# Two passes over the last four tiles of a projection stage

## The chip, the cores and the metric

The kernel runs on one core of a Trainium2 chip, as one program in one launch. The time is device time in microseconds (us), from three runs: a median of 3396.61 us, between 3395.56 and 3397.88. The engines are TensorE (PE: matmul; PEld: weight load), VectorE (DVE), ScalarE (ACT), GpSimd (POOL) and SyncE (SP, which here only starts transfers). Sixteen DMA engines move data between memory and the core's buffers; they are fed from a queue of SP (q1) and one of GpSimd (q0).

## The reference, cut to what matters

`z` is the input, of shape (1, 384, 384, 128). Two layers follow each other; all is float32.

```python
# layer 0
z_n = layernorm(z, norm_g, norm_b)
a = linear(z_n, Wa, ba) * sigmoid(linear(z_n, Wga, bga))
b = linear(z_n, Wb, bb) * sigmoid(linear(z_n, Wgb, bgb))
x = einsum('bijd,bjkd->bikd', a, b)
x = layernorm(x, normo_g, normo_b)
z1 = z + linear(x, Wo, bo) * sigmoid(linear(z_n, Wgo, bgo))
# layer 1 (pair = z1)
left = pair @ W_left + b_left + pair @ W_eq + b_eq
right_sum = sum(pair @ W_right + b_right, axis=2)
gate = sigmoid(pair @ W_gate + b_gate)
out = (left * right_sum * gate) @ W_out + b_out
return layernorm(out + pair, ln_scale, ln_bias)
```

## The kernel before

The kernel has three stages. The order of the instructions on each engine is the order in which the program writes them (`manual_schedule`, L37).

**Projection** (L93 to L321). x is cut into NT = 72 tiles of 128 rows by 16 columns (CX), each tile into four chunks of 4 columns (CT), so a step `s` (L183) handles one chunk and there are 288 steps. A step works on chunk `s` in its matmuls and on later chunks in the rest:

- `fetch` (L104) loads x three tiles ahead into a pool of four buffers (tag xt), on SP's queue; `statistics` (L121) takes mean and variance two tiles ahead on VectorE; `norm_factors` (L128) makes scale and offset one tile ahead on GpSimd; `normalise` (L139) writes zn on ScalarE, three chunks ahead.
- `turn` (L157) transposes the next chunk on TensorE into PSUM (ptr); `turned_out` (L166) copies it on ScalarE to zT.
- Four projections, `proj` (L199), of 128 x 512 each: ga, a, gb, b; `sigmoid` (L204) on ScalarE makes sga and sgb. VectorE forms at = (pa + bias) * sga (L218) and bt = (pb + bias) * sgb (L229). Four small matmuls pgo (L234) and gs (L236) make the output gate's argument; its sigmoid is taken one step later in `gate` (L173).
- All projections share a ring of six PSUM buffers (tag pk). The results at, gt, zb and bt have two buffers each.

Stores: at the end of a tile A is written from at (L222), and G from gt (L180), both from GpSimd's queue; Z, the input plus a bias, is made and written by GpSimd in `residual` (L149). B is written differently: bt gathers 64 columns, that is four tiles, and is written in four pieces of 32 rows (L243 to L249) on SP's queue. A piece goes out at the end of each tile; at the end of the last tile all pieces that are left go out at once (L245), these are the four of the last group.

**Product** (L387 to L452). For each of the 128 channels d, ad and bd are read back from A and B (`fetch`, L394; both on SP's queue, six channels ahead), multiplied (L412), and X, with running sums s1 and s2, is kept. s1 and s2 are cleared by GpSimd ahead of the stage (L332, L333).

**Output** (L457 to L593). The layer norm, the gate and layer 1, in a pipeline over rows.

The first product can start only when A and B are complete, since ad and bd of any channel hold values of every tile.

Of the kernel before, what the change touches and what calls it, by code (L numbers as in the profile page):

```python
# [8 lines left out]
FP = mybir.dt.float32  # L9
AF = mybir.ActivationFunctionType  # L10
# [9 lines left out]
def kernel(ctx: ExitStack, tc: tile.TileContext, ins, out: bass.AP):  # L20
# [66 lines left out]

    CG, CX, CT, BR = 64, 16, 4, 32  # L90
    TS = CX // CT
    NT = NB * (N // CX)
    with tc.tile_pool(name="wprep", bufs=6) as wp, tc.tile_pool(name="p1x", bufs=4) as px, tc.tile_pool(name="p1s", bufs=3) as ps, tc.tile_pool(  # L93
        name="p1o", bufs=2
    ) as po, tc.tile_pool(name="p1t", bufs=2, space=PSUM) as ppt, tc.tile_pool(
# [4 lines left out]
        def place(n):  # L100
            rb, c = divmod(n, N // CX)
            return rb * P, c * CX

        def fetch(n, parts=1):  # L104
            if n >= NT:
                return
            r0, c0 = place(n)
            xt = px.tile([P, CX, C], FP, tag="xt", name=f"xt_{n}")
            for k in range(0, CX, CX // parts):
                nc.sync.dma_start(  # L110
                    out=xt[:, k : k + CX // parts, :], in_=x[r0 : r0 + P, c0 + k : c0 + k + CX // parts, :]
                )
            tiles[n] = {
                "x": xt,
                "st": ps.tile([P, CX, 6], FP, tag="st", name=f"st_{n}"),
                "mv": ps.tile([P, CX, 2], FP, tag="mv", name=f"mv_{n}"),
                "rstd": ps.tile([P, CX], FP, tag="rstd", name=f"rstd_{n}"),
                "off": ps.tile([P, CX], FP, tag="off", name=f"off_{n}"),
            }
# [19 lines left out]
        def normalise(n, t, cs=range(CT)):  # L139
            if n >= NT:  # L140
                return
            g = tiles[n]
            for c in (t * CT + k for k in cs):
                nc.scalar.activation(  # L144
                    g["zn"][:, c, :], g["x"][:, c, :], AF.Identity,
                    bias=g["off"][:, c : c + 1], scale=g["rstd"][:, c : c + 1],
                )
# [9 lines left out]
        def turn(s):  # L157
            n, t = divmod(s, TS)
            if n >= NT:
                return  # L160
            ptr = ppt.tile([P, CT, P], FP, tag="ptr", name=f"ptr_{s}")
            for c in range(CT):
                nc.tensor.transpose(ptr[:, c, :], tiles[n]["zn"][:, t * CT + c, :], ident)  # L163
            turned[s] = ptr

        def turned_out(s):  # L166
            if s // TS >= NT:
                return
            zT = ps.tile([P, CT, P], FP, tag="zT", name=f"zT_{s}")
            nc.scalar.copy(zT, turned[s])  # L170
            turned[s] = zT

        def gate(s):  # L173
            n, t = divmod(s, TS)
            gs = gated.pop(s)
            gt = tiles[n]["gt"]
            nc.scalar.activation(gt[:, t * CT : (t + 1) * CT, :], gs, AF.Sigmoid)
            if t == TS - 1:
                r0, c0 = place(n)
                nc.gpsimd.dma_start(out=G[r0 : r0 + P, c0 : c0 + CX, :], in_=gt)  # L180
                tiles.pop(n - 1, None)

        def step(s):  # L183
            n, t = divmod(s, TS)
            r0, c0 = place(n)
            if t == 0:
                fetch(n + 3)
                if n:
                    norm_factors(n + 1)
                tiles[n]["at"] = po.tile([P, CX, P], FP, tag="at", name=f"at_{n}")  # L190
                tiles[n]["gt"] = po.tile([P, CX, C], FP, tag="gt", name=f"gt_{n}")
                if c0 % CG == 0:
                    bts[n // (CG // CX)] = po.tile([P, P, CG], FP, tag="bt", name=f"bt_{n}")
            at, bt = tiles[n]["at"], bts[n // (CG // CX)]
            k0 = c0 % CG + t * CT
            zT = turned.pop(s)
            ahead = (n + 1, t - 1) if t else (n, TS - 1)

            def proj(k):  # L199
                pk = ppp.tile([P, CT, P], FP, tag="pk", name=f"p{k}_{s}")  # L200
                nc.tensor.matmul(pk, lhsT=wT[k], rhs=zT, start=True, stop=True)  # L201
                return pk

            def sigmoid(k, pg):  # L204
                sg = ps.tile([P, CT, P], FP, tag="sg", name=f"sg{k}_{s}")
                nc.scalar.activation(sg, pg, AF.Sigmoid, bias=bcol["g" + k])  # L206
                return sg

            if n == 0:
                statistics(1, t)  # L210
                norm_factors(1, t * CT, t * CT + CT)
            statistics(n + 2, t)
            pga, pa = proj("ga"), proj("a")
            sga = sigmoid("a", pga)
            if s:
                gate(s - 1)
            normalise(*ahead, range(CT // 2))
            nc.vector.scalar_tensor_tensor(  # L218
                at[:, t * CT : (t + 1) * CT, :], pa, bcol["a"], sga, ALU.add, ALU.mult
            )  # L220
            if t == TS - 1:
                nc.gpsimd.dma_start(out=A[:, c0 : c0 + CX, r0 : r0 + P], in_=at)  # L222
            pgb = proj("gb")
            sgb = sigmoid("b", pgb)
            turn(s + 1)
            turned_out(s + 1)
            normalise(*ahead, range(CT // 2, CT))
            pb = proj("b")
            nc.vector.scalar_tensor_tensor(  # L229
                bt[:, :, k0 : k0 + CT].rearrange("d r c -> d c r"), pb, bcol["b"], sgb, ALU.add, ALU.mult  # L230
            )
            pgo = ppp.tile([P, CT, C], FP, tag="pk", name=f"pgo_{s}")
            for c in range(CT):
                nc.tensor.matmul(pgo[:, c, :], lhsT=zT[:, c, :], rhs=wT["go"], start=True, stop=True)  # L234
            gs = ps.tile([P, CT, C], FP, tag="gs", name=f"gs_{s}")
            nc.vector.tensor_tensor(gs, pgo, over(gate_bias, CT), ALU.add)  # L236
            gated[s] = gs
            if n == 1 and t < 3:
                residual(t)
            if n > 1 and t == 1:  # L240
                residual(n + 1)
            if k0 + CT == CG:
                b_out_of.extend((bt, r0, c0 + CX - CG, k) for k in range(0, P, BR))  # L243
            if t == TS - 1:
                store_b(len(b_out_of) if n == NT - 1 else 1)  # L245

        def store_b(pieces):
            for bt, r0, k0, r in b_out_of[:pieces]:
                nc.sync.dma_start(out=B[:, r0 + r : r0 + r + BR, k0 : k0 + CG], in_=bt[:, r : r + BR, :])  # L249
            del b_out_of[:pieces]  # L250
# [54 lines left out]
            if t == 1:  # L305
                prepare("go")
        for s in range(NT * TS):
            step(s)
            if s == TS:
                nc.vector.tensor_copy(ob_w, ob.to_broadcast([P, P]))  # L310
                prepare("o")
                nc.vector.tensor_scalar(center, ident, -1.0 / C, None, ALU.add)
                pc = ppp.tile([P, CT, P], FP, tag="pk", name="pc")[:, 0, :]
                nc.tensor.matmul(pc, lhsT=center, rhs=wT["o"], start=True, stop=True)
                nc.vector.tensor_copy(w_o0, pc)
                nc.vector.tensor_copy(w_o0[0:1, :], o_bias[0:1, :])
                nc.vector.tensor_tensor(w_left, w_left, w_eq, ALU.add)
                nc.vector.tensor_tensor(b_left, b_left, b_eq, ALU.add)
                nc.vector.tensor_scalar(b_right, b_right, float(N), None, ALU.mult)
                nc.vector.tensor_scalar(b_off, b_off, -1.0, None, ALU.mult)  # L320
        gate(NT * TS - 1)  # L321

# [4 lines left out]

    sums = ctx.enter_context(tc.tile_pool(name="sums", bufs=1, reuse_waits="tile"))  # L330
    x0, s1, s2, rs0 = (sums.tile([P, NB, N], FP, tag=k, name=k) for k in ("x0", "s1", "s2", "rs0"))
    nc.gpsimd.memset(s1, 0.0)  # L332
    nc.gpsimd.memset(s2, 0.0)  # L333
    LAST, AHEAD, R = 8, 6, 4
    pl = ctx.enter_context(tc.tile_pool(name="p3l", bufs=3, reuse_waits="tile"))
    group = {}
# [50 lines left out]
    with tc.tile_pool(name="p2", bufs=LAST, reuse_waits="tile") as p2, tc.tile_pool(  # L387
# [6 lines left out]
        def fetch(d):  # L394
            if d >= C:
                return
            ad = p2.tile([P, NB, N], FP, tag="ad", name=f"ad_{d}")
            bd = p2.tile([P, NB, N], FP, tag="bd", name=f"bd_{d}")
            nc.sync.dma_start(out=ad, in_=A[d].rearrange("(q p) i -> p q i", p=P))
            nc.sync.dma_start(out=bd, in_=B[d].rearrange("(q p) k -> p q k", p=P))  # L400
            factors[d] = ad, bd

# [26 lines left out]

        for d in range(AHEAD):  # L430
            fetch(d)
        for d in range(C - LAST):
            fetch(d + AHEAD)
            for ib in range(NB):
                product(d, ib)
# [194 lines left out]
```

## Time and profile before

| what | value |
|---|---|
| median of three runs | 3396.61 us |
| the profiled execution | 3399.26 us, its span 3397.5 us |
| PE busy | 3296.4 us (97% of the span) |
| DVE, ACT, POOL busy | 2673.1, 2307.0, 2089.3 us |
| mean granted TensorE clock | 0.988 |
| moved by DMA | 910.52 MB, 268 GB/s |
| one step on PE in the projection stage | 4.765 us |
| A, G, Z stores of 1 MB, median from issue to landing | 7.6, 8.8, 8.2 us |
| B store of 1 MB, median from issue to landing | 16.9 us |
| ad, bd loads, median from issue to landing | 7.3, 8.2 us |

The profile is one execution. Busy time is the time in which an engine has an instruction at work; a row of instructions has the line of the kernel, the engine, the operation and its tiles. A clock of 1.00 is TensorE's full speed. "Landing" is the end of a transfer, as the one who waits for it sees it. A DMA share of 1 means that all sixteen engines are busy. Rows of the timeline have their start and duration ahead, and behind, in brackets, what the engine waited for before.

### The profile page before, as it was taken

How to read it: one execution, taken by the hardware profiler on the slowest of the kernel's cores; microseconds unless marked ns; L12 is line 12 of the kernel's file. 1: busy time of each engine (PE TensorE's matmuls, PEld its weight loads, DVE VectorE, ACT ScalarE, POOL GpSimd, SP SyncE). 2: the span in 40 equal slices, each digit the busy share in tenths (PEclk: the TensorE clock that was granted, in tenths of full speed). 3: DMA queues.
4: the chain of work that ended last, by engine and by line, in shares of the span. 5: the costliest groups of instructions: out<-in, count | busy, mean ns of one | idle time of the engine just before them, and what ended most of it. 6: DMA issues, size and time to landing. Idle time of an engine off the chain costs nothing.

```text
span 3397.5 us, 53333 instructions
## 1 busy us (share of the span) xinstructions
PE 3296.4 (97%) x15581; PEld 2194.5 (65%) x15581; DVE 2673.1 (79%) x8605; ACT 2307.0 (68%) x5482; POOL 2089.3 (61%) x1562
## 2 busy tenths in 40 slices
PE   7999999999999999699999999899999999999997
PEld 4555555555555555355555555478888888888885
DVE  7777777777777777345555555599999999999998
ACT  5777877777877777422222222268888888888887
POOL 5555555555555555245555555338888888888887
PEclk9999999999999999899999999899999999999998
DMA  5888899999988899799999999667777777777773
GB/s 173 263 277 266 261 275 282 279 280 282 285 273 260 266 278 281 217 343 306 302 308 306 304 309 304 215 220 264 264 262 264 264 265 264 265 264 264 265 261 140
DMA packets 675330, 910.52 MB, mean 268 GB/s; under 512 B 319328, under 2 KB 616288, under 8 KB 647520
## 3 DMA queue, kind: packets, MB, share of 16 engines
q1 hardware_dynamic: 634000, 680.28, 63.4%
q0 software_dynamic: 40320, 226.51, 19.1%
q8 instruction: 126, 2.06, 0.2%
q14 instruction: 164, 1.34, 0.1%
q10 hardware_dynamic: 720, 0.33, 0.0%
HBM read 454.04 MB, written 452.98 MB: 267 GB/s over the span
## 4 chain that ended last, share of the span: by engine, by line
PE 91%; DVE 5%; POOL 1%; DMA 1%; issue 1%; SPq 0%; ACT 0%; POOLq 0%; ACTq 0%; DVEq 0%
PE pm L412 20%; PE pgo L234 7%; PE pga L201 7%; PE pa L201 7%; PE pgb L201 7%; PE pb L201 7%; PE pf L497 7%; PE py L507 7%; PE pleft L548 7%; PE pg L550 6%; PE ptr L163 4%; PE ptr L471 3%; DVE py L513 1%; DMA X<-xd 1%; DVE st L518 1%; DVE h L485 1%
## 5 line engine op out<-in xcount | busy, mean ns | idle before, releaser
L412 PE MATMUL pm<-bd,ad 128*128 128x384 f32 x2304 | 748.8, 489 | 32.0 <-DMA bd<-B 32.0
L412 PEld LDWEIGHTS pm<-bd,ad 128*128 128x128 f32 x2304 | 440.2, 191 | 339.2 <-issue 36.9
L427 POOL TENSOR_TENSOR s<-s,xd 128x384 f32<-128x384 f32 x381 | 380.3, 998 | 414.6 <-DVE xd L420 414.3
L425 ACT ACTIVATE sq<-xd 128x384 f32<-128x384 f32 x381 | 188.6, 495 | 566.0 <-DVE xd L420 566.0
L420 DVE TENSOR_TENSOR xd<-pm,x 128x384 f32<-128x384 f32 x381 | 212.2, 557 | 391.0 <-POOL s L427 321.6
L229 DVE SCALAR_TENSOR_TENSOR bt<-pb,c_L_conv_bb,sgb 128x512 f32<-128x512 f32 x288 | 321.0, 1115 | 247.6 <-ACT zT L170 239.1
L144 ACT ACTIVATE zn<-xt,off,rstd 128x128 f32<-128x128 f32 x1152 | 504.4, 489 | 15.1 <-POOL off L135 15.1
L540 ACT ACTIVATE res<-res,off,rs 128x128 f32<-128x128 f32 x1152 | 482.5, 486 | 18.4 <-POOL off L534 15.7
L513 DVE SCALAR_TENSOR_TENSOR py<-py,rs,gr 128x128 f32<-128x128 f32 x1152 | 431.4, 374 | 1.8 <-PE py L507 1.2
L222 POOL DMA_DIRECT2D A<-at x72 | 85.3, 1184 | 552.0 <-DVE at L218 552.0
L206 ACT ACTIVATE sga<-pga,c_L_conv_bga 128x512 f32<-128x512 f32 x288 | 197.9, 687 | 288.2 <-PE pga L201 288.2
L234 PEld LDWEIGHTS pgo<-wT_go,zT 128*128 128x128 f32 x2304 | 302.5, 192 | 137.7 <-issue 72.9
L518 DVE BATCH_NORM_STATS2 st<-res 128x6 f32<-128x128 f32 x1152 | 359.2, 313 | 0.3
L154 POOL TENSOR_TENSOR zb<-xt,r_L_conv_b_out 128x2048 f32<-128x2048 f32 x72 | 327.9, 4554 | 4.4 <-DMA Z<-zb 2.5
L580 POOL TENSOR_TENSOR res<-res,r_L_conv_ln_bias 128x1536 f32<-128x1536 f32 x94 | 324.7, 3455 | 7.4
L497 PE MATMUL pf<-w_o,h 128*128 128x128 f32 x2304 | 321.2, 276 | 6.1 <-ACT w_o L479 5.3
L579 POOL TENSOR_TENSOR res<-res,r_L_conv_ln_scale 128x1536 f32<-128x1536 f32 x94 | 325.4, 3461 | 0.1
L555 ACT ACTIVATE sg<-pg,c_L_conv_b_gate 128x384 f32<-128x384 f32 x384 | 223.0, 581 | 143.8 <-PE pg L550 90.9
L507 PE MATMUL py<-w_o,xr 128*128 128x128 f32 x2304 | 320.4, 275 | 0.0
L548 PE MATMUL pleft<-pairT,m_L_conv_W_left 128*128 128x384 f32 x768 | 313.0, 489 | 1.5 <-ACT pairT L473 1.3
L550 PE MATMUL pg<-pairT,m_L_conv_W_gate 128*128 128x384 f32 x768 | 311.1, 487 | 0.0
L125 DVE BATCH_NORM_STATS2 st<-xt 128x6 f32<-128x128 f32 x1152 | 305.6, 265 | 0.2 <-issue 0.2
(131 smaller groups left out, 6818.9 us busy)
## 6 DMA issues: line engine op xcount, KB each, us to landing
A<-at POOLq DMA_DIRECT2D x72, 1024.0 KB, 7.6
G<-gt POOLq DMA_DIRECT2D x72, 1024.0 KB, 8.8
Z<-zb POOLq DMA_DIRECT2D x72, 1024.0 KB, 8.2
B<-bt SPq DMA_DIRECT2D x72, 1024.0 KB, 16.9
ad<-A SPq DMA_DIRECT2D x128, 576.0 KB, 7.3
bd<-B SPq DMA_DIRECT2D x128, 576.0 KB, 8.2
xr<-X SPq DMA_DIRECT2D x96, 768.0 KB, 6.0
gr<-G SPq DMA_DIRECT2D x96, 768.0 KB, 7.6
```

The source lines that it names most:

```text
L144: nc.scalar.activation(g["zn"][:, c, :], g["x"][:, c, :], AF.Identity, bias=g["off"][:, c : c + 1], scale=g["rstd"][:, c : c + 1],)
L201: nc.tensor.matmul(pk, lhsT=wT[k], rhs=zT, start=True, stop=True)
L234: nc.tensor.matmul(pgo[:, c, :], lhsT=zT[:, c, :], rhs=wT["go"], start=True, stop=True)
L412: nc.tensor.matmul(pm, lhsT=ad[:, q, ib * P : (ib + 1) * P], rhs=bd[:, q, :], start=(q == 0), stop=(q == NB - 1),)
L427: nc.gpsimd.tensor_tensor(s1[:, ib, :], s1[:, ib, :], xd, ALU.add)
L497: nc.tensor.matmul(pf[:, q, :], lhsT=h[:, q * P : (q + 1) * P], rhs=w_o, start=True, stop=True)
L507: nc.tensor.matmul(py[:, q, :], lhsT=g["x"][:, i, q * P : (q + 1) * P], rhs=w_o0, start=True, stop=True)
L513: nc.vector.scalar_tensor_tensor(py[:, q, :], py[:, q, :], rs0[:, q, u : u + 1], g["g"][:, i, q, :], ALU.mult, ALU.mult)
L518: nc.vector.bn_stats(b["st"][:, k, q, :], b["res"][:, k, q, :])
L540: nc.scalar.activation(g["res"][:, i, q, :], g["res"][:, i, q, :], AF.Identity, bias=g["off"][:, i, q : q + 1], scale=g["rs"][:, i, q : q ...
L548: nc.tensor.matmul(pleft, lhsT=w_left, rhs=pairT, start=True, stop=True)
L550: nc.tensor.matmul(pg[:, 0:N], lhsT=w_gate, rhs=pairT, start=True, stop=True)
```

## The change

The last four tiles (68 to 71, the last group of B; steps S2 = 272 to 287) are handled in two passes. In the first pass each step does gb, b and the output gate, and the work ahead as before (statistics, factors, normalising, transposes), but neither ga nor a. The transposed chunk of these tiles is copied not into zT but into the tile's own x buffer, and stays there. After the first pass, whose end also sends off the B stores, the second pass runs ga and a for the 16 chunks from these buffers and stores A of the four tiles. The other 272 steps are written with new helper functions but keep their order.

Two more edits: ad of the first three channels (d below NB = 3) is read on GpSimd's queue in place of SP's, and the two clearings of s1 and s2 come after the first six fetches in the program.

```diff
+    S2 = (NT - CG // CX) * TS
...
         def turned_out(s):
             if s // TS >= NT:
                 return
-            zT = ps.tile([P, CT, P], FP, tag="zT", name=f"zT_{s}")
+            if s < S2:
+                zT = ps.tile([P, CT, P], FP, tag="zT", name=f"zT_{s}")
+            else:
+                n, t = divmod(s, TS)
+                zT = tiles[n]["x"][:, t * CT : (t + 1) * CT, :]
             nc.scalar.copy(zT, turned[s])
             turned[s] = zT
...
-                tiles.pop(n - 1, None)
...
+        def finish_a(s, pa, sga):
+            n, t = divmod(s, TS)
+            r0, c0 = place(n)
+            if t == 0:
+                tiles[n]["at"] = po.tile([P, CX, P], FP, tag="at", name=f"at_{n}")
+            at = tiles[n]["at"]
             nc.vector.scalar_tensor_tensor(
                 at[:, t * CT : (t + 1) * CT, :], pa, bcol["a"], sga, ALU.add, ALU.mult
             )
             if t == TS - 1:
                 nc.gpsimd.dma_start(out=A[:, c0 : c0 + CX, r0 : r0 + P], in_=at)
...
+        def step(s):
+            zT, ahead = begin(s)
+            pga, pa = project("ga", s, zT), project("a", s, zT)
+            sga = sigmoid("a", s, pga)
+            if s:
+                gate(s - 1)
+            normalise(*ahead, range(CT // 2))
+            finish_a(s, pa, sga)
+            sgb = sigmoid("b", s, project("gb", s, zT))
+            turn(s + 1)
+            turned_out(s + 1)
+            normalise(*ahead, range(CT // 2, CT))
+            finish_b(s, sgb, zT)
+
+        def first_pass(s):
+            zT, ahead = begin(s)
+            sgb = sigmoid("b", s, project("gb", s, zT))
+            turn(s + 1)
+            turned_out(s + 1)
+            gate(s - 1)
+            normalise(*ahead)
+            finish_b(s, sgb, zT)
+
+        def second_pass(s):
+            pga, pa = project("ga", s, turned[s]), project("a", s, turned[s])
+            finish_a(s, pa, sigmoid("a", s, pga))
...
         for s in range(NT * TS):
-            step(s)
+            step(s) if s < S2 else first_pass(s)
...
         gate(NT * TS - 1)
+        for s in range(S2, NT * TS):
+            second_pass(s)
...
-    nc.gpsimd.memset(s1, 0.0)
-    nc.gpsimd.memset(s2, 0.0)
...
-            nc.sync.dma_start(out=ad, in_=A[d].rearrange("(q p) i -> p q i", p=P))
+            queue = nc.gpsimd if d < NB else nc.sync
+            queue.dma_start(out=ad, in_=A[d].rearrange("(q p) i -> p q i", p=P))
...
         for d in range(AHEAD):
             fetch(d)
+        nc.gpsimd.memset(s1, 0.0)
+        nc.gpsimd.memset(s2, 0.0)
```

`begin` holds what a step did first (fetch, norm_factors, statistics); `finish_b` holds the b projection, bt, pgo, gs and what a step did after them; `project` and `sigmoid` are the old inner functions with the step as an argument.

More of the change, by code (lines that the diff above doesn't have):

```diff
@@ L180, in gate, with project, sigmoid, begin @@
                 nc.gpsimd.dma_start(out=G[r0 : r0 + P, c0 : c0 + CX, :], in_=gt)
-                tiles.pop(n - 1, None)
-        def step(s):
+        def project(k, s, zT):
+            pk = ppp.tile([P, CT, P], FP, tag="pk", name=f"p{k}_{s}")
+            nc.tensor.matmul(pk, lhsT=wT[k], rhs=zT, start=True, stop=True)
+            return pk
+        def sigmoid(k, s, pg):
+            sg = ps.tile([P, CT, P], FP, tag="sg", name=f"sg{k}_{s}")
+            nc.scalar.activation(sg, pg, AF.Sigmoid, bias=bcol["g" + k])
+            return sg
+        def begin(s):
             n, t = divmod(s, TS)
-            r0, c0 = place(n)
             if t == 0:
@@ L189, in step @@
                     norm_factors(n + 1)
-                tiles[n]["at"] = po.tile([P, CX, P], FP, tag="at", name=f"at_{n}")
                 tiles[n]["gt"] = po.tile([P, CX, C], FP, tag="gt", name=f"gt_{n}")
-                if c0 % CG == 0:
+                if n % (CG // CX) == 0:
                     bts[n // (CG // CX)] = po.tile([P, P, CG], FP, tag="bt", name=f"bt_{n}")
[L194 to L207, printed above, removed]
             if n == 0:
@@ L212, in step @@
             statistics(n + 2, t)
[L213 to L217, printed above, removed]
+            return turned[s], ((n + 1, t - 1) if t else (n, TS - 1))
+        def finish_a(s, pa, sga):
[4 more added lines that the diff above has]
+            at = tiles[n]["at"]
             nc.vector.scalar_tensor_tensor(
@@ L222, in step, with finish_b @@
                 nc.gpsimd.dma_start(out=A[:, c0 : c0 + CX, r0 : r0 + P], in_=at)
[L223 to L228, printed above, removed]
+        def finish_b(s, sgb, zT):
+            n, t = divmod(s, TS)
+            r0, c0 = place(n)
+            bt = bts[n // (CG // CX)]
+            k0 = c0 % CG + t * CT
+            pb = project("b", s, zT)
             nc.vector.scalar_tensor_tensor(
```

## The prediction

> **What bounds the kernel now.** Over the whole span the busy shares name TensorE (PE 97%), so I went to the slices first: PE is full but for the start, the end and the slice around 1400 us, where the projection stage ends. A table by stretches around that place, with PE busy in the third column and then the clock, DMA share and GB/s at the end:
>
> ```profile
> core 0: us, PE busy (x) PEld busy (x) DVE busy (x) ACT busy (x) POOL busy (x), PEclk, DMA share, GB/s
> 1334.60:1410.60 76.00, 75.96 (x318) 44.43 (x316) 49.21 (x113) 56.03 (x116) 33.48 (x26) 1.00 0.76 221
> 1410.60:1442.50 31.90, 0.00 (x0) 0.00 (x0) 0.79 (x2) 0.63 (x1) 2.61 (x3) 0.58 1.01 253
> 1442.50:1462.00 19.50, 19.45 (x55) 11.42 (x56) 4.64 (x9) 3.91 (x8) 4.97 (x5) 0.90 1.06 374
> ```
>
> The first stretch is exactly the last four tiles (16 steps; the timeline has pga of tile 68 at 1334.59 and the end of the last pgo at 1410.56): PE without a gap, DMA only 0.76 busy. Then PE does nothing for 31.9 us while the DMA engines are full. Who holds the end of that gap is in the chain of waits, in order of time:
>
> ```profile
> 1418.61 7.50 SPq L249
> 1426.11 0.04 issue
> 1426.15 11.49 DMA B<-bt
> 1437.64 0.02 issue
> 1437.66 0.03 SPq L400
> 1437.69 0.04 issue
> 1437.72 4.68 DMA bd<-B
> 1442.55 7.57 PE pm L412 x17
> ```
>
> The last group's four B stores (4 MB) can only leave when bt has its last column, at the very end. bd_0 waits for the last of them (1437.64), takes 4.9 us to the first product, and only then PE runs. So this gap belongs to transfers, and the question is how much PE work can be put beside them and what that work costs elsewhere.
>
> **The change, part by part.** Before, the stretch from the start of tile 68 to the first pm is 1442.55 - 1334.59 = 107.96 us. I rebuild it as T1 (first pass) + X (end of first pass to first pm).
>
> First pass on PE. One step is 4.765 us start to start (pga 1334.59, the next 1339.35): pga, pa, pgb, pb 0.86 each, the four transposes 0.44, pgo 0.89. Without pga and pa 3.04 us are left. But PE then no longer sets the pace alone. ScalarE's step, from the timeline (start, duration):
>
> ```profile
> 1354.71 0.69 ACT L206 ACTIVATE sga<-pga,c_L_conv_bga 128x512 f32<-128x512 f32 x1 [0.97 <-PE pga L201]
> 1355.30 0.62 ACT L177 ACTIVATE gt<-gs 128x512 f32<-128x512 f32 x1
> 1355.82 0.87 ACT L144 ACTIVATE zn<-xt,off,rstd 128x128 f32<-128x128 f32 x2
> 1356.59 0.67 ACT L206 ACTIVATE sgb<-pgb,c_L_conv_bgb 128x512 f32<-128x512 f32 x1
> 1357.15 0.57 ACT L170 COPY zT<-ptr 128x512 f32<-128x512 f32 x1
> 1357.62 0.88 ACT L144 ACTIVATE zn<-xt,off,rstd 128x128 f32<-128x128 f32 x2
> ```
>
> Its only wait is the 0.97 us in front of sga, so it works 4.765 - 0.97 = 3.80 us a step; taking sga out frees 0.59 (start to start), leaving 3.2. VectorE's step from the same timeline: bt 0.96, gs 0.60, four pairs of statistics 1.60, together 3.16 once at (0.74) is gone. ScalarE has normalising to do in 13 of the 16 steps; the last three are PE's 3.04, and the last lacks transposes. 13 x 3.2 + 3 x 3.04 - 0.4 = 50.3 us. As a bound from above, ScalarE's mean durations without overlap (0.67 + 0.57 + 0.62 + 4 x 0.49 = 3.82) give 58.4.
>
> To this comes a wait that did not show. The load of tile 71's x was issued at 1335.58 behind a B piece and landed 16.7 us later, at 1352.3:
>
> ```profile
> L110 SPq DMA_DIRECT2D xt<-in_x_dram x1: 7362/7362/7362, 1335.6 to 1335.6; - x1
> DMA to landing us min/median/max: 16.7/16.7/16.7
> ```
>
> Tile 69, whose steps take tile 71's statistics, used to start at 1353.65; now at 1334.6 + 4 x 3.2 = 1347.4, its statistics 0.9 later. VectorE stalls 4.0 us; queued behind the stalled statistics are bt and gs, then gate on ScalarE, which has about 1.3 us of room before gs is missed. I charge 2.7 us: T1 = 53.0, so the first pass ends at 1387.6. Bounds: 0 (the load comes earlier) to 4.0.
>
> The copies into x's buffers cost the same 0.57; they add a wait for GpSimd's zb, with gate, four zn and sgb queued behind it. For tile 69 zb ended at 1343.75 and the copy comes at about 1346, for tiles 70 and 71 the room is larger: nothing, and up to the 2 us of that room if GpSimd slips. No matmul, sigmoid or store is done twice, only their order differs; that the tile records are kept to the end costs nothing.
>
> Second pass: 16 x (0.86 + 0.86) = 27.5 us on PE; ScalarE 0.69 and VectorE 0.74 a step lie beside it. So PE's total is 53.0 + 27.5 = 80.5 against 76.0: 4.5 us are paid, to put 27.5 us of work into the gap.
>
> X is set by DMA. Count the bytes after the first pass: 4 MB of B as before, G of the last tile, and now all four A stores instead of one. Rates from the DMA view in stretches of one kind: B alone 3.03 MB in 14 us (1422 to 1436), so 4.19 MB take 19.4 us; G 0.77 MB in 2 us (1383 to 1385), so 2.7 us; A beside B 0.55 MB in 2 us, so 3.8 us each:
>
> ```profile
> q0 software_dynamic: 135, 0.55, 96.7%
> q1 hardware_dynamic: 75, 0.02, 4.5%
> ```
>
> (1376 to 1378, A of tile 69 on GpSimd's queue q0 while B is queued on SP's q1.) Sum 19.4 + 2.7 + 4 x 3.8 = 37.3 us. B's chain: issue 0.3 us after PE's end as before (1410.90 against 1410.56), first packet 2.0 later (an estimate: bd_0's 4.7 to landing less the time of its bytes and landing; 3.7 was seen behind an A store), 37.3, then 0.45 to the landing and 4.9 to the first pm: X = 45.0.
> A's chain: at of tile 71 is done 27.5 + 1.1 = 28.6 after the first pass, its store lands 9.1 later (the A store among B pieces at 1371), ad_0 lands 8.3 later (the ad row of that place): X = 46.1. The two nearly meet; I take X = 46.0. A's two at buffers make tile 70 wait for A of tile 68: issued at 8.0, landed at 17.1, wanted at 15.8. PE's six PSUM buffers cover that.
>
> The moved loads: ad_0 to ad_2 leave SP's queue for GpSimd's, behind the last A store that they wait for anyway, and bd_0 to bd_2 no longer queue behind them. No GpSimd row shows a load; between 4.7 (bd_0 alone) and 8.3 I took the row nearest in place, 8.3. The two memsets (1.08 each) now come behind these loads; the first addition into s1 comes after the second d, over 4 us after the first pm, so nothing; uncovered they'd cost 2.2.
>
> Sum: first pm at 1334.6 + 53.0 + 46.0 = 1433.6 instead of 1442.55, 8.9 us earlier. The stages after it are PE-bound and shift. PE still rests 1387.6 + 27.5 = 1415.1 to 1433.6, 18.5 us, so the restart at half clock (0.90 in the third stretch) is paid as before.
>
> **A rule against this.** The row above gives GpSimd's queue 96.7% of the engines and SP's 4.5%. The Trainium skill, "DMA: Bandwidth & Descriptors", section Queues, rings and completion order, says an engine goes round-robin between queue rows and drains a packet of some 9 to 17 descriptors at a turn. By that, turns of B's 256-byte pieces would weigh like A's packets, and A would take about 7.6 us, landing 13 after issue. Then at 71 waits for A 69 (14.8 + 13 = 27.8, done at 31.9), A 71 lands at 44.9, ad_0 at 53.2: a gain of 1.7 us. The measured row decides: 8.9.
>
> **The rivals.**
> Main (0.60): as summed, gain 6 to 12 us.
> More (0.12): the x load is early and A and B mix better (1357 to 1360 moved 0.99 MB in 3 us, 331 GB/s). T1 50.3, X 43: gain 14.7 us, 3381.9.
> Little (0.21): the first pass is a sum of durations, ScalarE at 3.82 a step, T1 58.4 and a first packet at 3.7: X 47.7, gain 1.9 us, 3394.7. For it: three engines within 5% of each other leave no room for waits. Against: ScalarE's single wait a step.
> Slower (0.07): A stores take turns as one more B piece. The place is the two at buffers: the end is 14.8 + L + 4.1 + L + 8.3, with L from issue to landing. Slower than before from 27.2 + 2L = 55.0, L = 13.9; by over 0.2% from L = 17.3; at 16.9 (B's median on the page) 6 us, at 20.1 (a B piece at 1357) 12 us, 3409. A's median of 7.9 speaks against it.
> That the gap isn't filled at all is excluded: nothing in the second pass waits for a transfer at its start.
>
> **How the numbers follow.** The profiled execution took 3399.26 (span 3397.5 plus 1.8), 2.65 above the median of 3396.61. 3399.26 - 8.9 = 3390.4; against the median 3387.7. The range runs from the second case, 3382, to the third, 3395. About 0.2%, 6.8 us, is what a measurement here can tell from no change. Of the main case some 0.07 falls below that: faster 0.65, same 0.28, slower 0.07.
>
> **What would show it.** Right: first-pass steps near 3.2 us and a wait of DVE st for xt of about 4 us in tile 69; PE full for 27 us after it; pm then waits some 18 us, for bd or ad within 1 us of each other; A lands within 9 us. Wrong: first-pass steps of 3.8 or more, at waiting for A over 5 us, or ad_0 alone arriving late.

## The result and the profile after

The changed kernel takes 3389.26 us (median of 14 runs, 3385.64 to 3391.25) against 3397.57 (14 runs of the kernel before, beside it): 8.3 us less, a ratio of 0.9976 with a 95% interval of 0.9969 to 0.9983. The forecast was 3387.7 and 8.9 us. The profiled execution of the changed kernel took 3391.23 us, its span is 3389.4.

The same table by stretches as before, cut where the first pass ends (1385.6), where PE ends (1413.8) and where the first product starts (1433.7):

```profile
1333.80:1385.60 51.80, 49.40 (x255) 32.94 (x254) 37.13 (x97) 45.20 (x100) 28.80 (x22) 1.00 0.88 264
1385.60:1413.80 28.20, 28.03 (x65) 11.71 (x63) 11.60 (x17) 11.51 (x17) 4.04 (x4) 1.00 0.96 237
1413.80:1433.70 19.90, 0.03 (x1) 0.00 (x0) 0.89 (x2) 0.00 (x0) 5.46 (x6) 0.60 0.89 255
1433.70:1453.20 19.50, 19.49 (x54) 11.38 (x55) 4.64 (x9) 3.91 (x8) 4.79 (x5) 0.89 1.06 374
```

PE used to be full for 76.0 us and then idle for 31.9. Now it is at work in 49.40 + 28.03 us, loses 2.4 us inside the first pass, and is idle for 19.9. During the second pass the DMA engines are 0.96 busy: this is the overlap that was bought. Tile 68 starts at 1333.78 in this execution, the first pm at 1433.71: a stretch of 99.93 us against 107.96, so 8.03 us of the 8.3 are here. What follows the first pm takes about the same: 1955.7 us to the end of the span, 1955.0 before.

The end of the gap, in the chain of waits in order of time:

```profile
1415.39 10.21 DMA A<-at
1425.67 0.51 issue
1426.20 7.47 DMA ad<-A
1433.71 11.48 PE pm L443 x28
```

It was B and bd_0 before; it is A and ad_0 now. And the waits of this place (who waited for what: in total, times, longest, in us):

```profile
PE pm L443 <- DMA ad<-A: 19.9, 1, 19.9
...
DVE at L220 <- DMA A<-at: 4.5, 1, 4.5
DVE st L128 <- DMA xt<-in_x_dram: 3.8, 1, 3.8
...
PE pgb L191 <- ACT xt L177: 1.7, 1, 1.7
```

The statistics wait of 3.8 us for the load of tile 71's x is the one that the kernel before did not show. How it reaches PE is read on ScalarE:

```profile
1347.28 0.69 ACT L196 ACTIVATE sgb<-pgb,c_L_conv_bgb 128x512 f32<-128x512 f32 x1
1347.85 0.59 ACT L177 COPY xt<-ptr 128x512 f32<-128x512 f32 x1
1348.32 0.65 ACT L184 ACTIVATE gt<-gs 128x512 f32<-128x512 f32 x1
1348.85 1.66 ACT L147 ACTIVATE zn<-xt,off,rstd 128x128 f32<-128x128 f32 x4
1350.38 0.69 ACT L196 ACTIVATE sgb<-pgb,c_L_conv_bgb 128x512 f32<-128x512 f32 x1
1350.95 0.59 ACT L177 COPY xt<-ptr 128x512 f32<-128x512 f32 x1
1354.68 0.63 ACT L184 ACTIVATE gt<-gs 128x512 f32<-128x512 f32 x1 [3.13 <-DVE gs L239]
```

From one sgb to the next it is 3.10 us with no wait at all, against 3.05 on PE: ScalarE has become the engine that sets the step, and after the stall PE's steps are 3.11 us too. So when gt has to wait 3.13 us for gs, which VectorE could not make behind its stalled statistics, nothing later takes that back. Of this PE loses 0.65 us in front of a pb and 1.75 in front of a pgb.

### The profile page after: what moved, and what is told of

It is laid out like the page before. It is cut to its first block, busy times and chain, and to the rows that moved or that the text cites. A ratio compares the mean times of both kernels' runs of the same rounds, so it can differ in the third digit from the quotient of the medians.

```text
span 3389.4 us, 53346 instructions
## 1 busy us (share of the span) xinstructions
PE 3298.0 (97%) x15581; PEld 2195.0 (65%) x15581; DVE 2672.4 (79%) x8605; ACT 2306.0 (68%) x5482; POOL 2091.0 (62%) x1565
## 4 chain that ended last, share of the span: by engine, by line
PE 81%; DVE 13%; DMA 2%; POOL 2%; issue 2%; ACT 1%; SPq 0%; POOLq 0%; ACTq 0%; DVEq 0%
PE pm L443 19%; PE pgo L237 7%; PE pgb L191 7%; PE pb L191 7%; PE pga L191 7%; PE pa L191 7%; PE py L540 5%; PE pleft L581 5%; PE pf L530 5%; PE pg L583 5%; PE ptr L166 4%; DVE py L546 3%; PE ptr L504 3%; DVE st L551 2%; DVE h L518 2%; DVE res L531 2%
## 5 line engine op out<-in xcount | busy, mean ns | idle before, releaser
L443 PE MATMUL pm<-bd,ad 128*128 128x384 f32 x2304 | 749.4, 489 | 19.9 <-DMA ad<-A 19.9
L546 DVE SCALAR_TENSOR_TENSOR py<-py,rs,gr 128x128 f32<-128x128 f32 x1152 | 388.8, 337 | 1.8 <-PE py L540 1.2
L237 PEld LDWEIGHTS pgo<-wT_go,zT 128*128 128x128 f32 x2176 | 285.7, 192 | 130.0 <-issue 67.4
L551 DVE BATCH_NORM_STATS2 st<-res 128x6 f32<-128x128 f32 x1152 | 316.7, 276 | 0.3
```

What stands on the lines that cost most here:

```text
L443: nc.tensor.matmul(pm, lhsT=ad[:, q, ib * P : (ib + 1) * P], rhs=bd[:, q, :], start=(q == 0), stop=(q == NB - 1),)
L546: nc.vector.scalar_tensor_tensor(py[:, q, :], py[:, q, :], rs0[:, q, u : u + 1], g["g"][:, i, q, :], ALU.mult, ALU.mult)
L551: nc.vector.bn_stats(b["st"][:, k, q, :], b["res"][:, k, q, :])
```

## The experiments

The numbers to compare are the time, and, since single executions differ by a few us, the stretch from tile 68's first matmul to the first pm, which each trace shows. The stretch is that of one execution too: the traced ones of the kernel before, the changed kernel, e2 and e7 are 1.7 to 2.0 us above their medians, the others within 1.3 us. In the table "below before" is the median against the runs of the kernel before on the same chip.

| kernel | stretch, us | median, us | below before, us | ratio, 95% interval |
|---|---|---|---|---|
| before | 107.96 | 3397.57 | | |
| changed | 99.93 | 3389.26 | 8.3 | 0.9976 (0.9969 to 0.9983) |
| e1: ad on SP | 97.99 | 3389.72 | 7.7 | 0.9976 (0.9967 to 0.9985) |
| e2: three tiles | 99.59 | 3389.46 | 8.0 | 0.9975 (0.9967 to 0.9984) |
| e3: two tiles | 102.23 | 3392.92 | 4.5 | 0.9988 (0.9981 to 0.9994) |
| e4: x load first | 96.02 | 3386.45 | 11.0 | 0.9970 (0.9958 to 0.9981) |
| e5: the two small edits alone | 110.43 | 3400.68 | -3.2 | 1.0009 (1.0001 to 1.0018) |
| e6: e4 and ad on SP | 94.78 | 3385.18 | 12.3 | 0.9963 (0.9950 to 0.9977) |
| e7: three tiles, ad on SP | 96.54 | 3385.92 | 11.6 | 0.9966 (0.9954 to 0.9979) |
| e8: A stores on SP | 104.29 | 3394.61 | 2.9 | 0.9991 (0.9983 to 0.9999) |
| e9: three A stores early | 96.95 | 3387.81 | 10.3 | 0.9971 (0.9960 to 0.9983) |

Two theories stood at first. The chain theory: what is left of the gap is a chain of landings, A of tile 71, then ad_0. The drain theory: it is the bytes of A and B that are still to be written when the first pass ends. A third, the cover theory, was the plain reading of the change: the more PE work is laid into the gap, the better.

**e1, the loads moved back.**

```diff
-            queue = nc.gpsimd if d < NB else nc.sync
+            queue = nc.sync
```

> The changed kernel with ad_0 to ad_2 back on SP's queue. Chain theory: what remains of the gap is the chain A of tile 71 lands, ad_0 is issued, ad_0 lands, and on GpSimd's queue the last step takes 7.5 us where bd_0 on SP's took 3.9. On SP it should take about 4.5 to 5, so the first pm comes some 2.5 us sooner: 3386.8 us, 10.8 below before. Drain theory: the bytes of A and B behind the last matmul set the end whatever queue reads: no change from the changed kernel, 3389.3. A third view, in favour of the move: on SP bd_0 is queued behind ad_0, which costs up to 1 us: 3390.

In the trace the first pm comes 1.9 us sooner, released by bd_0:

```profile
1426.39 5.11 DMA bd<-B
1431.49 0.14 issue
1431.63 8.41 PE pm L443 x17
```

ad_0 is issued at 1425.80 and bd_0 0.6 later, and both are there 5.8 us after that first issue, where ad_0 alone took 7.5 on GpSimd's queue. The median did not follow (3389.72). 1.9 us lies within the interval, which is about 3 us to each side, and the two traces are not of equally fast executions (2.0 us above the median for the changed kernel, 0.2 for e1). So the time leaves this open; e6 and e7 come back to it.

**e2 and e3, fewer tiles.**

```diff
-    S2 = (NT - CG // CX) * TS
+    S2 = (NT - 3) * TS
```

> Two passes over the last three tiles in place of four. Drain and chain theory: the first pass ends 3.6 us later (4 steps of 1.72 us come back into it, less the 2.5 us stall for x of tile 71 and the longer steps), but one A store of 3.8 us leaves the drain and the second pass is 6.9 us shorter, so the A chain ends 3.7 us earlier: first pm 3.7 us sooner, 3385.6 us, 12 below before. Cover theory (each us of PE work laid into the gap is a us gained): 6.9 us less cover cost 3 to 4 us: 3393.

> Two passes over the last two tiles. Drain and chain theory: B lands 32.6 us after the first pass and sets the end now; first pm 0.8 us sooner than with four tiles: 3388.5 us. Cover theory: 13.8 us of cover less than with four: 3396.

All four figures missed. Three tiles are as good as four, neither better nor worse, and two lose 3.7 us. Cover alone is not the measure: e2 gives up 6.9 us of PE work in the gap (PE is idle for 23.4 us instead of 19.9) at no cost in time. But my sum was 3.4 us too good as well, and the trace says where. B landed at 1424.5, as worked out, and then:

```profile
1424.47 0.02 issue
1424.48 0.03 SPq L431
1424.51 0.04 issue
1424.55 7.53 DMA bd<-B
1432.09 0.14 issue
1432.22 7.78 PE pm L443 x14
```

bd_0 takes 7.53 us in place of 3.9. The DMA view of 1424.5 to 1428, right after its issue, has the queues:

```profile
q0 software_dynamic: 312, 1.28, 99.2%
q1 hardware_dynamic: 2, 0.00, 0.8%
```

A is complete sooner here, so ad_0 to ad_2 were issued at 1420.4 from GpSimd's queue, 4.2 us ahead of bd_0, and they go ahead of it: two of the three are not needed yet. In e3 the three loads (issued at 1421.9, before B landed at 1429.7) ran into the B stores in the same way, and bd_0 took 5.4 us. That made a third thing to test: GpSimd's queue goes ahead of SP's, whatever it carries. In this form it is wrong, and the changed kernel's own trace shows it: there SP's loads, issued first, held up GpSimd's (below, "The moved loads").

**e4, the x load ahead of a B piece.**

```diff
-                store_b(len(b_out_of) if n == NT - 1 else 1)
+                store_b(len(b_out_of) if n == NT - 1 else {NT - 5: 0, NT - 4: 2}.get(n, 1))
```

> The changed kernel with the B piece at the end of tile 67 held back to the end of tile 68 (two pieces there), so that the load of tile 71's x is first in SP's queue. If the stall of VectorE for this load costs what the trace shows (PE waits 0.65 and 1.75 us), the first pass is 2.4 us shorter and everything after it moves up: 3386.9 us. Rival: later transfers set the end and the piece that was held back only makes them later: no change, 3389.3.

The time is as worked out, 11.0 us below before; the stretch is 3.9 us shorter, more than the 2.4 of the stall. The first pass has lost its hole. A row of the table by stretches (it reaches half a microsecond into the second pass) has PE busy from end to end:

```profile
1333.10:1382.20 49.10, 49.10 (x256) 32.82 (x255) 37.81 (x98) 45.13 (x100) 28.84 (x22) 1.00 0.88 257
```

The last pgo of the first pass ends at 1381.75, so this pass took 48.7 us in place of 51.9: 3.2 us. Of these, 2.4 are the two waits of PE, and PE's steps of 3.11 us after the stall are 3.05 here up to tile 70. The second pass takes the same, the gap is 0.6 us shorter, which I did not take apart. No cost of the later B pieces shows.

**e5, the small edits alone.** The kernel before, with only the moved loads and clearings.

```diff
-            nc.sync.dma_start(out=ad, in_=A[d].rearrange("(q p) i -> p q i", p=P))
+            queue = nc.gpsimd if d < NB else nc.sync
+            queue.dma_start(out=ad, in_=A[d].rearrange("(q p) i -> p q i", p=P))
```

> The kernel before with only the two small edits: ad_0 to ad_2 read on GpSimd's queue, the clearings of s1 and s2 behind the fetches. Precedence theory (what GpSimd's queue holds goes ahead of what SP's holds, as the A stores did): the three loads, 1.77 MB or some 5 us, run ahead of the B stores, which land 4 to 5 us later, while bd_0 saves about 1 us without ad_0 before it: 3401, 3 to 4 us slower than before. Rival: the loads use time that is free anyway: no change, or 1 us faster (3396.5).

3.2 us slower, the stretch 2.5 us longer. The chain of waits:

```profile
1429.02 10.67 DMA B<-bt
1439.69 0.02 issue
1439.70 0.03 SPq L399
1439.73 0.04 issue
1439.77 3.90 DMA bd<-B
1443.68 0.14 issue
1443.81 6.38 PE pm L411 x13
```

B was issued at 1409.70 and landed 30.0 us later; before it was 26.7 (1410.90 to 1437.64). The three loads, issued at 1414.8, took that time from B; bd_0 itself landed 0.8 us faster. In this kernel nobody could use A early, since B was last. The clearings are done at 1419.2, 24 us ahead of the first pm.

**e6, both corrections.** The edits of e1 and e4 together.

> Four tiles in two passes, the x load ahead of the held-back B piece, and ad on SP's queue. If both effects are real and independent, the stretch from tile 68's start to the first pm is 96.0 less 1.9, 94.1 us, and the time 3384.5. Rival: the move of ad is worth nothing in time: 3386.4, as with the x load alone.

12.3 us below before, the lowest median of all, and a stretch of 94.78 where 94.1 was worked out. Against e4 it is 1.2 us in the trace and 1.3 in the medians, within the intervals: alone it would not show that the move is worth something.

**e7, three tiles with ad on SP.** The edits of e1 and e2.

> Two passes over three tiles, ad on SP's queue. With three tiles bd_0 took 7.5 us to land while ad_0 to ad_2 ran ahead of it from GpSimd's queue; from SP's it should take under 6, so the first pm comes 1.8 us sooner than in the run with three tiles: a stretch of 97.8 from tile 68's start, 3387.5 us. Rival: other transfers filled that time, no change: 3389.5.

bd_0 takes 4.90 us instead of 7.53, the stretch is 3.1 us shorter (1.8 were expected), the median 3.5 us lower than with three tiles; the slowest run of e7 (3387.67) is faster than the fastest of e2 (3388.27). So the moved loads cost that much where they reach the DMA engines first, and with this the sum for three tiles holds (3385.6 was worked out in e2, 3385.92 is measured).

**e8, the A stores of the second pass on SP's queue.**

```diff
-                nc.gpsimd.dma_start(out=A[:, c0 : c0 + CX, r0 : r0 + P], in_=at)
+                queue = nc.sync if n >= NT - 4 else nc.gpsimd
+                queue.dma_start(out=A[:, c0 : c0 + CX, r0 : r0 + P], in_=at)
```

> The changed kernel with the four A stores of the second pass on SP's queue, behind the B stores. It tests what the change rests on, that these stores overtake B. If they do so only because they stand in another queue, A of tile 68 now lands after all of B, about 28 us into the second pass; at of tile 70 waits for it, PE with it for about 10 us; A of tile 71 lands near 47 and the first pm comes some 53 us after the first pass, 5 us later than in the changed kernel: 3394 to 3396. If the order of the queues doesn't matter because the bytes set the end: within 1.5 us of the changed kernel, 3388 to 3390.5.

5.4 us of the gain are gone (3394.61). The waits show the mechanism of the slower case, at its place:

```profile
DVE at L220 <- DMA A<-at: 13.9, 2, 13.1
...
PE pa L191 <- DVE at L220: 7.0, 1, 7.0
```

The first A store can only be issued at 1401.67, when SP has placed all of B; at of tile 70 waits 13.1 us for it, and PE 7.0 us for that. The same bytes, in the other queue, give back most of what the change won.

**e9, three A stores taken out of the second pass.** Places 68 to 70 of A get a second copy of tiles 64 to 66, stored in the ordinary steps: these parts of A hold other values than they should.

```diff
-                nc.gpsimd.dma_start(out=A[:, c0 : c0 + CX, r0 : r0 + P], in_=at)
+                if n not in (NT - 4, NT - 3, NT - 2):
+                    nc.gpsimd.dma_start(out=A[:, c0 : c0 + CX, r0 : r0 + P], in_=at)
+                if n in (NT - 8, NT - 7, NT - 6):
+                    r4, c4 = place(n + 4)
+                    nc.gpsimd.dma_start(out=A[:, c4 : c4 + CX, r4 : r4 + P], in_=at)
```

> The changed kernel with the A stores of tiles 68 to 70 left out of the second pass; their places are filled instead by storing the at of tiles 64 to 66 a second time, in the ordinary steps before, so these three parts of A hold another tile's values. 3 MB leave the drain, 11 us of DMA time. Two-chains theory: B lands 11 us earlier, but A of tile 71 cannot be issued before PE has made it, 29.7 us after the first pass; it lands some 8 to 9 us later and ad_0 takes 5 to 7.5: first pm 2.5 to 4 us sooner than in the changed kernel, 3385 to 3387. Drain alone: the first pm comes 8 us or more sooner, 3381 or less.

B now lands at 1411.2, 13.6 us earlier counted from tile 68's start, and bd_0 is there at 1415.1. Yet the first pm comes only 3.0 us sooner:

```profile
1415.99 6.06 DMA A<-at
...
1422.63 7.00 DMA ad<-A
1429.63 0.04 issue
1429.68 5.41 PE pm L447 x8
```

Without B beside it A of tile 71 lands in 6.06 us instead of 10.21. The stretch hides a part of this: VectorE waits 6.4 us for x where it was 3.8, which I put down to the extra stores, and the first pass takes 54.6 us where it took 51.9. Counted from the end of the first pass, B lands 16.4 us earlier and the first pm comes 5.7 us sooner. The median, 3387.81, is 0.8 us above the band of the two-chains theory. PE waits for ad_0 until 14.6 us after bd_0 is there, so the drain alone is refuted: two chains end the gap, B's 3.8 us shorter than A's in the changed kernel, and taking away one leaves the other.

## Why the prediction was right, step by step

**The first pass** was worked out at 53.0 us and took 51.9. Its step was said to be 3.2 us; it is 3.05 in tile 68, PE's own pace, and 3.10 from sgb to sgb on ScalarE. The estimate came from busy time less one start-to-start gap and was 3% high. The rival "Little", a step of 3.82 us from mean durations, is refuted by ScalarE's rows above: each instruction starts before the one ahead of it has ended.

**The stall for tile 71's x** was found from a landing time alone and held: VectorE waits 3.83 us (4.0 worked out), PE loses 2.4 (2.7), and e4 gives it back.

**The second pass** took 28.2 us for 27.5: two small waits of pa for a free buffer, 0.5 us together. Behind them stands VectorE, which waited 4.3 us for A of tile 68 to leave its buffer (the profile puts this down to pa, but the store landed at 1404.5 and at starts at 1404.6) and 4.5 us for A of tile 69, where 1.3 us had been worked out for the first. The PSUM buffers covered most of this for PE, as was said, but not for at.

**A's and B's chains** were put at 46.1 and 45.0, so that X was 46.0; it was 48.05. B landed 39.9 us after its issue and bd_0 took 3.9: the B side would have allowed a first pm at about 1430. The term that was too small is A's landing in the tail, 10.2 us where 9.1 was taken (its four stores: 10.8, 11.2, 9.8, 10.2), with an issue 1.1 us later than worked out (29.7 us after the first pass; in e9, where at waits for no store of A, it is 28.6 as in the sum) and 0.6 us between A's landing and the issue of ad_0, which the sum did not have; ad_0's own landing was 0.8 us shorter than charged. bd and ad were to arrive within 1 us of each other; they are 3.8 apart. "ad_0 alone arriving late" stood among the signs of being wrong, and it came; the two waits of at stayed under their 5 us. The balance of the two chains was not met, though the sum was.

**A's precedence** was the step on which the forecast hung, where the rule of equal turns (the Trainium skill, "DMA: Bandwidth & Descriptors", Queues, rings and completion order) would, as the prediction weighed it, have left 1.7 us of gain. The DMA view of 1407 to 1410, with A of tile 69 under way and B queued (queue, packets, MB, share of the engines' time):

```profile
q0 software_dynamic: 196, 0.80, 93.8%
q1 hardware_dynamic: 195, 0.05, 7.7%
```

Once it moves, A has the engines nearly to itself, as the row of before said. But the count of packets, 196 and 195, is that of equal turns: to this extent the trace agrees with the skill's turns between queues. What does not hold is the weight that the prediction gave to a turn, in which B's small pieces would have come up to A's packets. A packet of A is 4 KB here (0.80 MB in 196), one of B 256 bytes (0.05 MB in 195), so with equal turns nearly all the time goes to A. The row of before has 135 packets against 75 only because B had none left after the first half (from 1376 to 1377 it is 65 against 75); e5's loads beside B's stores have 183 against 182 from 1422 to 1424. So A is not preferred; its pieces are larger. And it is some 5 us from its issue to that, when B's pieces are under way: A of tile 69, issued at 1400.55, is still absent from the view of 1405 to 1406, where B moves 0.21 MB in 1 us. That delay was in the 9.1 us and not in the words.

**The moved loads** were charged a landing of 8.3 us for ad_0 and nothing else. 7.47 us came, but not for a reason that stands in the sum: the 8.3 is from a load on SP's queue behind B's stores, and after 1426 no store was left. What filled the 7.47 is other loads. bd_0 was issued at 1425.92, ad_0 at 1426.20, and behind bd_0 on SP's queue came bd_1, bd_2, ad_3 and bd_3. The DMA view of 1427 to 1430:

```profile
q1 hardware_dynamic: 660, 0.99, 97.5%
q0 software_dynamic: 2, 0.01, 1.0%
```

So for nearly 4 us ad_0 stood behind loads of which only bd_0 was needed next. From about 1430 the queues took turns:

```profile
q0 software_dynamic: 168, 0.70, 71.1%
q1 hardware_dynamic: 168, 0.24, 27.3%
```

(1431 to 1433.7; a packet of ad on q0 is 4 KB, one on q1 about 1.5.) In e2 it was the other way round, ad_0 to ad_2 were there first and bd_0 stood behind them. In both it is the queue whose loads were issued first that kept the engines, for about 3.5 us after the issue of the other's; why a new transfer takes so long to come in is open, and no run here tests it. With ad and bd on one queue, in the order in which the channels need them, this goes away. What the move cost: 3.1 us with three tiles (e2 against e7), 2.5 when done without the two passes (e5), and by single traces 1.9 in the changed kernel (e1) and 1.2 with the x load first (e4 against e6). That 8.3 was near is luck.

Of the sum, then, 8.9 us, the first pass gave 1.1 us more and X took 2.05 back, which leaves the 8.0 us by which the stretch moved. The mechanism was right (work beside the stores, A past B, the stall for x); that the number came within 1 us of it owes something to errors that cancel.

## What to carry to other kernels

When a stage ends on transfers, moving matmuls behind the last store is worth not the matmuls moved but the distance to the next chain: add up the bytes left and the landing of the last store, and stop where the two meet (three tiles did what four did). A step that loses a matmul has another engine as its pace, and loads that came just in time before come late: look for the landing times just ahead of the first user. Neither queue went ahead as such: with both at work the one with larger packets got most of the time, and a load that had just been issued stood behind the other queue's loads for some 3.5 us. So keep the loads that are needed together in one queue, in the order of need, and ask of each transfer in another queue what it will stand behind.

## What the runs showed of the hardware

The restart of TensorE's clock is not of one length. With PE at work from the first pm on, e2 stays at half clock for 6.1 us, e3 for 3.4; the other traces lie between. The table by stretches of e2 (the granted clock stands behind the five engines; the first rows reach a little beyond the change):

```profile
1432.20:1438.50 6.30, 6.28 (x10) 3.49 (x11) 0.00 (x0) 0.48 (x1) 0.00 (x0) 0.51 1.07 374
1438.50:1442.00 3.50, 3.50 (x12) 2.09 (x11) 0.00 (x0) 0.96 (x2) 0.00 (x0) 1.00 1.06 373
```

and of e3:

```profile
1435.20:1438.70 3.50, 3.50 (x6) 1.97 (x7) 0.00 (x0) 0.00 (x0) 0.00 (x0) 0.53 1.07 378
1438.70:1442.00 3.30, 3.30 (x11) 1.91 (x11) 0.00 (x0) 0.96 (x2) 0.00 (x0) 1.00 1.06 373
```

At half speed the 2.7 us between them are 1.4 us of matmuls, after idle times of 23.4 and 26.3 us. So two executions of kernels that differ by about 1 us at such a gap can come out alike. What follows the first pm is longest in e2 and shortest in e3 (1957.3 and 1954.6 us to the end of the span). In e1's trace the half clock lasts 5.4 us, in the changed kernel's 4.4, and what follows takes 0.8 us more: so much of its 1.9 us is lost again. Whether this is also why e1's median did not follow was not tried.
